# State scans of a four-layer image model: half of the products with B move to the matrix engine

## The chip, the core and the metric

The program runs on one core of a Trainium2 chip. The core has five instruction queues that run side by side: the matrix engine (PE in the profile, with PEld for its weight loads), the vector engine (DVE), the activation engine (ACT), the general engine (POOL) and SP, which here only issues transfers. Two on-chip memories matter: SBUF, which every engine can use, and PSUM, which the matrix engine writes and which DVE and ACT can read and write. The metric is device time of the whole program in microseconds. The kernel before takes 34342.57 us (median of 3 runs, 34341.05 to 34345.31).

## The reference, cut to what matters

Four layers are added one after the other to an image of 256 x 256 positions with 128 channels. Layer 1 is a selective state scan, and the change lies there. It has four scan directions (k = 0 to 3: by rows, by columns, and both backwards), 256 inner channels and 16 states for each channel, over 65536 positions:

```python
def step(h, inp):
    d_t, x_t, B_t, C_t = inp
    dA = jnp.exp(d_t[..., None] * As)
    h = dA * h + (d_t * x_t)[..., None] * B_t[:, :, None, :]
    y = jnp.einsum('bkdn,bkn->bkd', h, C_t)
    return (h, y)
```

For each channel d and state n, a = exp(delta * A) multiplies the old state, and delta * x * B is added. B and C depend on position and state alone, not on the channel. y is the sum over the 16 states of h * C.

## The kernel before

`scan_stream` does the scans. Channels lie on the 128 partitions, in two halves (dh = 0 and 1), and positions run along the free dimension. The work is cut into 512 chunks: 4 directions times 128 chunks of 512 positions. A chunk has 8 slots (NG); a slot is four states (G) of one half. Slot j has half j % 2 and states 4 * (j // 2) onwards, so halves alternate and states rise.

In every slot the engines share the work so:

- ACT computes a = exp(delta * A) for four states, 512 positions each (L787), into the PSUM tiles `das`. Two states lie behind each other in one tile, so that one scan instruction runs over both; a is set to 0 at the seam, and a one-element ACT instruction (L791) adds the second state's carry to its first product.
- DVE runs two scan instructions (L802), each over 1024 elements: a from PSUM, the products `db` from SBUF, the result `h` to SBUF.
- POOL multiplies h with C (`c_product`, L817, 2048 elements) from SBUF to SBUF.
- PE transposes and adds the four products for the chunk's y in PSUM (`sums`, L827, 16 instructions of 128 columns for a slot), two slots later.
- The products db = B * (delta * x) for a slot are one instruction of 2048 elements (`b_product`, L769): in slots 2, 4 and 6 on POOL, in the five others on DVE. For DVE delta * x lies in PSUM (`mm` for half 0, `du1` for half 1), and B, spread over all partitions by a transfer, in SBUF (`bb`). For POOL ACT copies delta * x into SBUF (`dus`, L758).

Once a chunk, delta and delta * x of the next one are made in small steps between the slots: PE (`dt`, L704; `soft_sum`, L729), ACT (`soft_abs`, `soft_exp`, `delta_copy`), and DVE (`delta_x`, L747, one instruction for each half). B and C come from PE (`xproj`), go out to DRAM (`xd_copy`), and come back in eight transfers of 1024 KB a chunk (`load_b`, `load_c`), each row repeated on all partitions.

The order on each engine is the program's order (`manual_schedule`): every engine runs its instructions in the order in which the loop at L906 issues them, and waits where data or a buffer is not ready. `h` has three buffers, `hc` three, `db` five, `bb` and `cc` three each. In PSUM, y takes two tiles of 2 KB a partition, `das` two of 4 KB, `mm` and `du1` 2 KB each.

Of the kernel before, what the change touches and what calls it, by code (L numbers as in the profile page):

```python
# [576 lines left out]
def scan_stream(c, xc2, y, w):  # L577
# [8 lines left out]
    G, BL, NG = 4, 1024, 8  # L586
    R = y[1].shape[3]
    NW = BL // S
    on_pool = (2, 4, 6)
    b_order = {0: (3,), 1: (4,), 2: (5,), 3: (6, 7), 4: (8,), 6: (10,)}  # L590
# [5 lines left out]
    with ExitStack() as a:  # L596
        st = a.enter_context(tc.tile_pool(name="l1b_st", bufs=1))
        io = a.enter_context(tc.tile_pool(name="l1b_io", bufs=2))
        bcp = a.enter_context(tc.tile_pool(name="l1b_bc", bufs=3))
        wk = a.enter_context(tc.tile_pool(name="l1b_wk", bufs=2))  # L600
        dram = a.enter_context(tc.tile_pool(name="l1b_dr", bufs=4, space=DRAM))
        ps1 = a.enter_context(tc.tile_pool(name="l1b_p1", bufs=1, space=PSUM))
        states = [st.tile([P, 2, 16], F32, name=f"l1b_state{k}") for k in range(4)]

        xds = [st.tile([64, CH], F32, name=f"l1b_xd{i}") for i in range(3)]
        for s in states:
            nc.vector.memset(s, 0.0)
        for xd in xds:
            nc.vector.memset(xd[32:64], 1.0)
        ys = [ps1.tile([P, CH], F32, name=f"l1b_y{dh}") for dh in range(2)]  # L610
        das = [ps1.tile([P, 2, CH], F32, name=f"l1b_da{i}") for i in range(2)]


        mm = ps1.tile([P, CH], F32, name="l1b_mm")
        du1 = ps1.tile([P, CH], F32, name="l1b_du")
        blocks, bcs, bbs, ccs, soft, dls, dbs, hs, hcs, yts = ({} for _ in range(10))
# [49 lines left out]

        def xproj(ch):
            if ch >= N:
                return
            k = chunks[ch][0]  # L670
            for dh in range(2):
                nc.tensor.matmul(  # L672
                    du1[:40],
                    w["xproj"][:, dh, k, :],
                    in_block(blocks[ch][0], ch, dh),
                    start=dh == 0,
                    stop=dh == 1,
                )

        def xd_copy(ch):  # L680
            if ch >= N:
                return
            xd = xds[ch % 3]
            nc.scalar.copy(xd[:40], du1[:40])
            bc = bcs[ch] = dram.tile([32, CH], F32, name="l1b_bc")
            nc.sync.dma_start(bc, xd[8:40])

        def load_b(m):
            if m < 4 * N:
                n0 = m % 4 * G  # L690
                bb = bbs[m] = bcp.tile([P, G, CH], F32, name="l1b_bb")
                nc.sync.dma_start(bb, bcs[m // 4][n0 : n0 + G][None].to_broadcast([P, G, CH]))

        def load_c(m):
            if m < 4 * N:
                n0 = 16 + m % 4 * G
                cc = ccs[m] = bcp.tile([P, G, CH], F32, name="l1b_cc")
                nc.sync.dma_start(cc, bcs[m // 4][n0 : n0 + G][None].to_broadcast([P, G, CH]))


# [11 lines left out]
        def soft_abs(ch):  # L712
            if ch >= N:
                return
            soft[ch] = wk.tile([P, CH], F32, name="l1b_tail", bufs=1)
# [17 lines left out]
        def delta_copy(ch, dh):  # L733
# [4 lines left out]
            dl = dls[ch, dh] = wk.tile([P, CH], F32, name=f"l1b_dl{dh}")  # L738
            nc.scalar.copy(dl, mm)  # L739
            af = dls[ch, dh, "first"] = wk.tile([P, 16], F32, name=f"l1b_af{dh}")  # L740
# [3 lines left out]
        def delta_x(ch, dh):  # L744
            if ch >= N:
                return
            nc.vector.tensor_tensor(  # L747
                like_block(du1 if dh else mm, ch),
# [5 lines left out]
        def du_copy(ch):  # L754
            if ch >= N:
                return
            dls[ch, "du"] = wk.tile([P, CH], F32, name="l1b_dus")
            nc.scalar.copy(dls[ch, "du"], mm)  # L758

        def b_product(g):  # L760
            ch, j = divmod(g, NG)
            if ch >= N:
                return
            db = dbs[g] = wk.tile([P, G, CH], F32, name="l1b_db", bufs=5)
            if j in on_pool:
                eng, du = nc.gpsimd, dls[ch, "du"]
            else:
                eng, du = nc.vector, du1 if j % 2 else mm
            eng.tensor_tensor(db, bbs[g // 2], du[:, None, :].to_broadcast([P, G, CH]), ALU.mult)  # L769

        def scans(g, extras):
            ch, j = divmod(g, NG)
            k, dh, n0, rev = chunks[ch][0], j % 2, j // 2 * G, chunks[ch][0] >= 2
            db = dbs.pop(g).rearrange("p g t -> p (g t)")
            h = hs[g] = wk.tile([P, G, CH], F32, name="l1b_h", bufs=3)
            hf = h.rearrange("p g t -> p (g t)")
            dl, af = dls[ch, dh], dls[ch, dh, "first"]
            mid = CH - 1 if rev else CH
            for i in range(2):
                one, two = n0 + 2 * i + rev, n0 + 2 * i + 1 - rev  # L780
                da = das[i].rearrange("p g t -> p (g t)")
                if g == 0 or ch == N // 2 and j == 0:
                    nc.vector.memset(da[:, mid : mid + 1], 0.0)
                for n in (one, two):
                    o = n % 2 * CH
                    lo, hi = (0, CH) if n == one else (0, CH - 1) if rev else (1, CH)
                    nc.scalar.activation(  # L787
                        da[:, o + lo : o + hi], dl[:, lo:hi], AF.Exp, scale=w["A"][:, k, dh, n : n + 1]
                    )
                first = db[:, 2 * i * CH + mid : 2 * i * CH + mid + 1]  # L790
                nc.scalar.activation(  # L791
                    first,
                    states[k][:, dh, two : two + 1],
                    AF.Identity,
                    scale=af[:, two : two + 1],
                    bias=first,
                )
                sl = slice(2 * i * CH, 2 * i * CH + 2 * CH)
                h_, a_, d_ = hf[:, sl], da, db[:, sl]
                if rev:  # L800
                    h_, a_, d_ = h_[:, ::-1], a_[:, ::-1], d_[:, ::-1]
                nc.vector.tensor_tensor_scan(  # L802
                    h_, a_, d_, states[k][:, dh, one : one + 1], ALU.mult, ALU.add
                )
# [4 lines left out]

        def keep_state(g):  # L810
            ch, j = divmod(g, NG)
            k, dh, n0 = chunks[ch][0], j % 2, j // 2 * G
            nc.scalar.copy(states[k][:, dh, n0 : n0 + G], hs[g][:, :, 0 if k >= 2 else CH - 1])  # L813

        def c_product(g):
            hc = hcs[g] = wk.tile([P, G, CH], F32, name="l1b_hc", bufs=3)
            nc.gpsimd.tensor_tensor(hc, hs[g], ccs[g // 2], ALU.mult)  # L817
            hs.pop(g - 1, None)

        def y_turn(ch, dh):  # L820
            if ch < 0:
                return
            yt = yts[dh] = wk.tile([P, CH], F32, name="l1b_yt", bufs=1)
            nc.scalar.copy(yt, ys[dh])  # L824

        def turned(to, b, part, start, stop):
            nc.tensor.matmul(  # L827
                to[:, bass.ts(b, P)],
                part,
                c.ident,  # L830
                start=start,
                stop=stop,
                is_transpose=True,
                skip_group_check=True,
            )

        def y_start(ch, dh):
            k = chunks[ch][0]
            xc, yo = blocks[ch]
            for b in range(CH // P):  # L840
                if k == 2:
                    turned(ys[dh], b, in_block(yo, ch, dh)[:, bass.ts(b, P)], b == 0, True)
# [10 lines left out]
        def sums(g):  # L853
            ch, j = divmod(g, NG)
            new = chunks[ch][0] % 2 == 1
            if j < 2 and not new:
                y_start(ch, j)
            hc = hcs.pop(g)
            for i in range(G):
                for b in range(CH // P):  # L860
                    turned(
                        ys[j % 2], b, hc[:, i, bass.ts(b, P)], new and j < 2 and i + b == 0, True
                    )

        def y_back(ch, dh):
# [6 lines left out]
            for b in range(CH // P):  # L872
                turned(ys[dh], b, yts[dh][:, bass.ts(b, P)], b == 0 and not add, True)
# [17 lines left out]
        for m in range(3):  # L891
            load_b(m)
            load_c(m)
        for dh in range(2):
# [6 lines left out]
            if dh == 0:  # L901
                du_copy(0)
            b_product(dh)
        b_product(2)
        load_b(3)
        for ch in range(N):  # L906
            nxt = ch + 1
            for s in range(NG):
                g = NG * ch + s
                if s == 3 and ch % 2 == 0:  # L910
                    load_y(ch + 2)
                if s == 5 and ch % 2 == 1:
                    load_x(ch + 3)
                if s == 4:
                    delta_x(nxt, 0)
                for j in b_order.get(s, ()):
                    b_product(NG * ch + j)
                extras = [[], []]
                if s == 1:
                    extras = [  # L920
                        [lambda: y_turn(ch - 1, 0), lambda: y_back(ch - 1, 0)],
                        [lambda: soft_abs(nxt), lambda: y_out(ch - 1, 0)],
                    ]
                if s == 2:
                    extras = [
                        [lambda: y_turn(ch - 1, 1), lambda: y_back(ch - 1, 1)],
                        [lambda: soft_exp(nxt), lambda: y_out(ch - 1, 1)],
                    ]
                if s == 3:
                    extras[1] = [lambda: delta_copy(nxt, 0)]  # L930
                if s == 4:
                    extras[0] = [lambda: du_copy(nxt)]
                if s == 5:
                    extras = [[lambda: soft_abs(nxt)], [lambda: soft_exp(nxt)]]
                if s == 6:
# [860 lines left out]
```

## Time and profile before

The profiled execution took 34336.33 us, of which its span covers 34334.6. Its scan stage runs from the first scan instruction (3912.9 us) to the end of the last one (29617.4 + 2.3 us): 25706.8 us, or 50.21 us for each of 512 chunks. What is left, 8629.5 us, is the other layers and the ends of layer 1.

| engine, whole span | busy us | share | instructions |
|---|---|---|---|
| PE | 23728.7 | 69% | 108660 |
| DVE | 31153.8 | 91% | 23679 |
| ACT | 23345.7 | 68% | 48143 |
| POOL | 27466.5 | 80% | 6996 |

A line of the profile's groups names the source line, the engine, the operation, what it writes and reads, its shape and its count; after the bar stand busy time in us and the mean duration of one in ns, and then the time for which the engine stood idle just before such instructions, with what ended it. Busy time counts overlapped parts of neighbouring instructions once, so busy time over count is the pace in a row, a little under the mean duration.

### The profile page before, as it was taken

How to read it: one execution, taken by the hardware profiler on the slowest of the kernel's cores; microseconds unless marked ns; L12 is line 12 of the kernel's file. 1: busy time of each engine (PE TensorE's matmuls, PEld its weight loads, DVE VectorE, ACT ScalarE, POOL GpSimd, SP SyncE). 2: the span in 40 equal slices, each digit the busy share in tenths (PEclk: the TensorE clock that was granted, in tenths of full speed). 3: DMA queues.
4: the chain of work that ended last, by engine and by line, in shares of the span. 5: the costliest groups of instructions: out<-in, count | busy, mean ns of one | idle time of the engine just before them, and what ended most of it. 6: DMA issues, size and time to landing. Idle time of an engine off the chain costs nothing. (4 is left out here: it accounts for less than half of the span.)

```text
span 34334.6 us, 330861 instructions
## 1 busy us (share of the span) xinstructions
PE 23728.7 (69%) x108660; PEld 15714.0 (46%) x108660; DVE 31153.8 (91%) x23679; ACT 23345.7 (68%) x48143; POOL 27466.5 (80%) x6996
## 2 busy tenths in 40 slices
PE   7999766666666666666666666666666666799877
PEld 3554444444444444444444444444444444434444
DVE  6668999999999999999999999999999999873699
ACT  3667777777777777777777777777777777532477
POOL 2446899999999999999999999999999999720000
PEclk9999877777777777777777777777887787899999
DMA  3113455555555555555555555555555555675111
GB/s 141 45 45 123 185 190 189 191 190 190 189 191 189 189 190 190 190 189 191 195 201 199 201 200 200 199 202 200 200 202 200 201 199 201 209 233 160 68 35 33
DMA packets 2076823, 5952.61 MB, mean 173 GB/s; under 512 B 115207, under 2 KB 1379608, under 8 KB 1499222
## 3 DMA queue, kind: packets, MB, share of 16 engines
q1 hardware_dynamic: 1939122, 5860.18, 47.2%
q10 hardware_dynamic: 135972, 71.27, 0.7%
q8 instruction: 855, 14.01, 0.2%
q14 instruction: 874, 7.16, 0.1%
HBM read 5238.41 MB, written 692.58 MB: 173 GB/s over the span
## 5 line engine op out<-in xcount | busy, mean ns | idle before, releaser
L802 DVE TENSOR_TENSOR_SCAN l1b_h<-l1b_da,l1b_state,l1b_db 128x1024 f32<-128x1024 f32 x8192 | 18847.8, 2337 | 678.8 <-ACT l1b_db L791 594.3
L817 POOL TENSOR_TENSOR l1b_hc<-l1b_h,l1b_cc 128x2048 f32<-128x2048 f32 x4096 | 18480.3, 4537 | 430.8 <-DVE l1b_h L802 430.8
L787 ACT ACTIVATE l1b_da<-l1b_dl,l_alog 128x512 f32<-128x512 f32 (+1 forms) x16384 | 11298.8, 690 | 2793.1 <-DVE l1b_h L802 2484.9
L827 PE MATMUL l1b_y<-ident,l1b_hc 128*128 128x128 f32 x65536 | 10636.3, 331 | 3479.7 <-POOL l1b_hc L817 3474.4
L827 PEld LDWEIGHTS l1b_y<-ident,l1b_hc 128*128 128x128 f32 x65536 | 9760.0, 175 | 5869.2 <-POOL l1b_hc L817 4330.6
L769 POOL TENSOR_TENSOR l1b_db<-l1b_bb,l1b_dus 128x2048 f32<-128x2048 f32 x1536 | 6965.5, 4535 | 46.6 <-DMA l1b_bb<-l1b_bc 46.6
L769 DVE TENSOR_TENSOR l1b_db<-l1b_bb,l1b_du 128x2048 f32<-128x2048 f32 x2048 | 4656.9, 2274 | 35.1
L704 PE MATMUL l1b_mm<-l1b_xd,l_dtw 41*128 41x512 f32 x2048 | 1753.9, 950 | 3303.1 <-ACT l1b_dus L758 2746.7
L791 ACT ACTIVATE l1b_db<-l1b_state,l1b_db,l1b_af 128x1 f32<-128x1 f32 x8192 | 3045.4, 372 | 0.0
L813 ACT COPY l1b_state<-l1b_h 128x4 f32<-128x4 f32 x4095 | 788.9, 193 | 2387.2 <-DVE l1b_h L802 2386.4
L729 PE MATMUL l1b_mm<-l1b_tail,ident 128*128 128x512 f32 x2048 | 1470.0, 808 | 911.4 <-ACT l1b_tail L724 908.9
L704 PEld LDWEIGHTS l1b_mm<-l1b_xd,l_dtw 41*128 41x128 f32 x2048 | 438.1, 266 | 3576.6 <-ACT l1b_dus L758 2867.5
L332 POOL TENSOR_TENSOR l0b_e<-l0b_e,l0b_den 128x1024 f32<-128x1024 f32 x512 | 969.0, 1893 | 1372.9 <-DVE l0b_den L331 726.4
L827 PE MATMUL l1b_y<-ident,l1b_yt 128*128 128x128 f32 x4096 | 877.7, 352 | 1448.2 <-ACT l1b_yt L824 1448.2
L827 PEld LDWEIGHTS l1b_y<-ident,l1b_yt 128*128 128x128 f32 x4096 | 597.2, 177 | 1890.0 <-ACT l1b_yt L824 1709.1
L758 ACT COPY l1b_dus<-l1b_mm 128x512 f32<-128x512 f32 x512 | 299.6, 585 | 1387.7 <-DVE l1b_db L769 1387.3
L769 DVE TENSOR_TENSOR l1b_db<-l1b_bb,l1b_mm 128x2048 f32<-128x2048 f32 x512 | 1171.0, 2287 | 18.2 <-ACT l1b_dus L758 0.7
L672 PE MATMUL l1b_du<-l1b_xc,l_xproj 128*40 128x512 f32 x2048 | 1158.0, 694 | 32.4 <-DMA l1b_xc<-l_xc 31.6
L308 DVE CUSTOM_DVE_ANT_0 l0b_e<-l0b_sc,l0b_bias 128x256 f32<-128x256 f32 x2048 | 745.4, 420 | 414.8 <-PE l0b_sc L297 411.4
L323 ACT ACTIVATE l0b_e<-l0b_e,l0b_top 128x256 f32<-128x256 f32 x2048 | 1012.1, 498 | 0.9 <-DVE l0b_top L308 0.9
L739 ACT COPY l1b_dl<-l1b_mm 128x512 f32<-128x512 f32 x1024 | 587.6, 574 | 520.4 <-DVE l1b_du L747 516.1
L729 PEld LDWEIGHTS l1b_mm<-l1b_tail,ident 128*128 128x128 f32 x2048 | 386.9, 237 | 1069.6 <-ACT l1b_tail L724 1065.5
(282 smaller groups left out, 30409.0 us busy)
## 6 DMA issues: line engine op xcount, KB each, us to landing
l1b_bb<-l1b_bc SPq DMA_DIRECT2D x2048, 1024.0 KB
l1b_cc<-l1b_bc SPq DMA_DIRECT2D x2048, 1024.0 KB
l1b_xc<-l_xc SPq DMA_DIRECT2D x128, 1024.0 KB
l_y<-l1b_yo SPq DMA_DIRECT2D x128, 1024.0 KB
l1b_xc<-l_xct SPq DMA_DIRECT2D x256, 512.0 KB
l_y<-l1b_yo SPq DMA_DIRECT2D x256, 512.0 KB
l_xc<-l1a_o SPq DMA_DIRECT2D x64, 1024.0 KB
l_xct<-l1a_ot SPq DMA_DIRECT2D x16, 4096.0 KB
```

Of the source, the lines that this page charges most:

```text
L323: nc.scalar.activation(e[:, i], e[:, i], AF.Exp, scale=-1.0, bias=top[:, i : i + 1], accum_out=den[:, i : i + 1],)
L332: nc.gpsimd.tensor_tensor(e, e, den[:, :, None].to_broadcast([P, 4, S]), ALU.mult)
L672: nc.tensor.matmul(du1[:40], w["xproj"][:, dh, k, :], in_block(blocks[ch][0], ch, dh), start=dh == 0, stop=dh == 1,)
L704: nc.tensor.matmul(mm, w["dt"][:, chunks[ch][0], dh * P : dh * P + P], xds[ch % 3][0:41], start=True, stop=True,)
L729: nc.tensor.matmul(mm, c.ident, soft.pop(ch), start=False, stop=True, skip_group_check=True)
L769: eng.tensor_tensor(db, bbs[g // 2], du[:, None, :].to_broadcast([P, G, CH]), ALU.mult)
L787: nc.scalar.activation(da[:, o + lo : o + hi], dl[:, lo:hi], AF.Exp, scale=w["A"][:, k, dh, n : n + 1])
L791: nc.scalar.activation(first, states[k][:, dh, two : two + 1], AF.Identity, scale=af[:, two : two + 1], bias=first,)
L802: nc.vector.tensor_tensor_scan(h_, a_, d_, states[k][:, dh, one : one + 1], ALU.mult, ALU.add)
L813: nc.scalar.copy(states[k][:, dh, n0 : n0 + G], hs[g][:, :, 0 if k >= 2 else CH - 1])
L817: nc.gpsimd.tensor_tensor(hc, hs[g], ccs[g // 2], ALU.mult)
L827: nc.tensor.matmul(to[:, bass.ts(b, P)], part, c.ident, start=start, stop=stop, is_transpose=True, skip_group_check=True,)
```

## The change

In each chunk, states 4 to 7 and 12 to 15 (q = 1 and 3, where q numbers the groups of four states) get their products with B from PE. The slots are put in a new order, in which a slot with products from a DVE or POOL instruction (q even) and one with products from PE (q odd) alternate; slot s of a chunk is `SLOTS[s]`, a pair (q, dh).

- For a slot with q odd, `fill` issues eight matmuls. The stationary operand is delta * x, turned so that positions are on partitions (`duts`; turned by PE in `du_turn`, copied by ACT in `du_copy`). The moving operand is `diag`: for 64 positions a diagonal pattern with the four values of B at each position. The result, 128 channels x 64 positions x 4 states, lands in the PSUM tile `dbt` with the four states next to each other at each position. `dbt` takes 8 KB of PSUM a partition and has one buffer.
- The pattern is made by transfers: B is turned by PE (`b_turn`), copied by ACT (`b_copy`), written to the diagonal places of a DRAM tile (`far`) in four transfers of 16-byte pieces a chunk, and loaded back (`load_d`, two of 512 KB a chunk) for the next chunk but one.
- The scans of a slot with q odd are four of 512 elements instead of two of 1024: a from SBUF (`dad`), products from `dbt` at every fourth element, h to SBUF. There is no seam, so no one-element ACT instruction.
- The scans of a slot with q even stay two of 1024, but a (`das`) now lies in SBUF beside db.
- delta * x is written to SBUF (`dus`) for both halves. The four product instructions that remain a chunk are two on DVE (for slots 4 and 0) and two on POOL (for slots 6 and 2). B's broadcast loads fall from four to two a chunk.
- `hc` has two buffers instead of three, `bb` two, `db` three.

```diff
-    on_pool = (2, 4, 6)
-    b_order = {0: (3,), 1: (4,), 2: (5,), 3: (6, 7), 4: (8,), 6: (10,)}
+    SLOTS = [(0, 0), (1, 0), (0, 1), (1, 1), (2, 0), (3, 0), (2, 1), (3, 1)]
+    HQ = P // 2
+    NB = CH // P
...
+        das = [st.tile([P, 2, CH], F32, name=f"l1b_das{i}") for i in range(2)]
+        dad = [st.tile([P, CH], F32, name=f"l1b_dad{i}") for i in range(4)]
+        dus = [st.tile([P, CH], F32, name=f"l1b_du{dh}") for dh in range(2)]
+        duts = [st.tile([P, NB, P], F32, name=f"l1b_dut{dh}") for dh in range(2)]
+        diag = {q: st.tile([P, NB, HQ, G], F32, name=f"l1b_diag{q}") for q in (1, 3)}
...
-        das = [ps1.tile([P, 2, CH], F32, name=f"l1b_da{i}") for i in range(2)]
+        dbt = ps1.tile([P, CH, G], F32, name="l1b_dbt")
         mm = ps1.tile([P, CH], F32, name="l1b_mm")
-        du1 = ps1.tile([P, CH], F32, name="l1b_du")
+        mi = ps1.tile([P, CH], F32, name="l1b_mi")
...
+        def load_d(ch, q):
+            if ch < N:
+                nc.sync.dma_start(diag[q], far[q, ch % 3])
...
             nc.vector.tensor_tensor(
-                like_block(du1 if dh else mm, ch),
+                like_block(dus[dh], ch),
                 like_block(mm, ch),
...
+        def b_product(ch, s, eng):
             if ch >= N:
                 return
...
+            q, dh = SLOTS[s]
+            db = dbs[NG * ch + s] = wk.tile([P, G, CH], F32, name="l1b_db", bufs=3)
+            du = dus[dh][:, None, :].to_broadcast([P, G, CH])
+            eng.tensor_tensor(db, bbs[ch, q], du, ALU.mult)
+
+        def fill(g):
+
+            s = g % NG
+            q, dh = SLOTS[s]
+            v = dbt.rearrange("p (a r q e) n -> p a r e q n", r=2, q=HQ, e=2)
+            for n in range(2 * NB):
+                b, r = n // 2, n % 2
+                rows = slice(r * HQ, r * HQ + HQ)
+                nc.tensor.matmul(
+                    v[:, b // 2, r, b % 2],
+                    duts[dh][rows, b],
+                    diag[q][rows, b],
...
+                if q % 2 == 0:
+                    both_scans(g, i)
+                else:
+                    for j in (2 * i, 2 * i + 1):
+                        da, n = dad[j], n0 + j
+                        nc.scalar.activation(da, dl, AF.Exp, scale=w["A"][:, k, dh, n : n + 1])
+                        h_, a_, d_ = h[:, j], da, dbt[:, :, j]
+                        if rev:
+                            h_, a_, d_ = h_[:, ::-1], a_[:, ::-1], d_[:, ::-1]
+                        nc.vector.tensor_tensor_scan(
+                            h_, a_, d_, states[k][:, dh, n : n + 1], ALU.mult, ALU.add
+                        )
...
+                if s == 0:
...
+                    fill(g + 1)
+                    du_turn(ch, 1)
...
+                if s == 2:
+                    fill(g + 1)
...
+                if s == 3:
+                    b_product(ch, 4, nc.vector)
...
                 if s == 4:
                     delta_x(nxt, 0)
...
+                    fill(g + 1)
...
+                if s == 5:
                     extras = [
...
+                        [lambda: soft_abs(nxt)],
+                        [lambda: du_copy(nxt, 0), lambda: soft_exp(nxt)],
                     ]
...
                 if s == 6:
+                    fill(g + 1)
...
                 if s == 7:
...
+                    extras = [
+                        [lambda: delta_x(nxt, 1), lambda: b_product(nxt, 0, nc.vector)],
+                        [lambda: delta_copy(nxt, 1), lambda: b_copy(ch + 2)],
+                    ]
+                    b_turn(ch + 2)
                 scans(g, extras)
...
+                sums(g - 2)
+                if s == 4:
+                    b_product(ch, 6, nc.gpsimd)
+                if s == 7:
+                    b_product(nxt, 2, nc.gpsimd)
                 c_product(g)
```

`both_scans` holds the old body of `scans` unchanged, with `das` and `db` as its operands. `extras[i]` are run behind the first or the second half of a slot's scans.

## The prediction

> **What bounds the kernel now.** I read the scan stage alone, since the change touches nothing else: 50.21 us for each of 512 chunks, with 8629.5 us of the profiled execution's 34336.33 around it. First the busy time of the engines in a stretch of that stage (the columns after the stretch are its length, then busy us with instruction counts for PE, PEld, DVE, ACT and POOL, then the granted clock, DMA share and GB/s), then the groups.
>
> ```profile
> 10000.00:16000.00 6000.00, 3730.82 (x17800) 2759.12 (x17801) 5831.01 (x2749) 4319.71 (x8844) 5900.48 (x1315) 0.74 0.53 190
> ```
>
> ```profile
> L802 DVE TENSOR_TENSOR_SCAN l1b_h<-l1b_da,l1b_state,l1b_db 128x1024 f32<-128x1024 f32 x8192 | 18847.8, 2337 | 678.8 <-ACT l1b_db L791 594.3
> L817 POOL TENSOR_TENSOR l1b_hc<-l1b_h,l1b_cc 128x2048 f32<-128x2048 f32 x4096 | 18480.3, 4537 | 430.8 <-DVE l1b_h L802 430.8
> ...
> L769 POOL TENSOR_TENSOR l1b_db<-l1b_bb,l1b_dus 128x2048 f32<-128x2048 f32 x1536 | 6965.5, 4535 | 46.6 <-DMA l1b_bb<-l1b_bc 46.6
> L769 DVE TENSOR_TENSOR l1b_db<-l1b_bb,l1b_du 128x2048 f32<-128x2048 f32 x2048 | 4656.9, 2274 | 35.1
> ```
>
> DVE is busy for 97% of the stretch and POOL for 98%. Two engines bound the stage together, so work must leave both. By busy time over count: a scan 2.30 us, a C product 4.51, a B product 4.53 on POOL and 2.28 on DVE, `delta_x` (L747) 0.67. A chunk is then 16 x 2.30 + 5 x 2.28 + 2 x 0.67 = 49.5 us on DVE and 8 x 4.51 + 3 x 4.53 = 49.7 on POOL.
>
> The last thing to see is how steady these two engines are beside each other. For one line of code, minimum, median and maximum duration in ns:
>
> ```profile
> L802 DVE TENSOR_TENSOR_SCAN l1b_h<-l1b_da,l1b_state,l1b_db x8192: 2319/2343/2354, 3912.9 to 29617.4; 128x1024 f32<-128x1024 f32 x200
> ```
>
> The spread over 8192 scans is 35 ns, although POOL runs nearly without pause. Every DVE instruction of this stage streams one operand from PSUM (`das`, `du1`, `mm`) and one from SBUF. Further on, where layer 1 ends, the trace has a DVE instruction (L1100) with two streams from SBUF, and POOL sometimes runs an add (L1029) at the same time. Its 256 instances take 737/744/2049 ns (minimum, median, maximum). Three looks at one meeting, in order of time; the second figure is the duration:
>
> ```profile
> 29826.09 1.54 POOL L1029 TENSOR_TENSOR l1c_y<-l1c_y,l1c_yt 128x512 f32<-128x512 f32 x1 [7.80 <-DMA l1c_y<-l_y]
> ...
> 29826.51 1.68 DVE L1100 SCALAR_TENSOR_TENSOR l1c_y<-l1c_y,l1c_lnb,l1c_sz 128x512 f32<-128x512 f32 x1
> ```
>
> ```profile
> 29828.10 2.02 DVE L1100 SCALAR_TENSOR_TENSOR l1c_y<-l1c_y,l1c_lnb,l1c_sz 128x512 f32<-128x512 f32 x1
> ```
>
> ```profile
> 29826.09 6.91 POOL L1029 TENSOR_TENSOR l1c_y<-l1c_y,l1c_yt 128x512 f32<-128x512 f32 x4 [7.80 <-DMA l1c_y<-l_y]
> ```
>
> The first DVE instruction starts inside POOL's first add and ends 0.56 us after that add's end (29827.63). The second takes 2.02 us and ends at about 29830.1, 0.5 us after POOL's second add. POOL's four adds take 6.91 us; two undisturbed ones take 3.01 (at 29815.28), so four would be 6.02, and each DVE instruction cost POOL 0.44 us. They take turns: each holds the other off for a whole instruction. In the same place L1093, with one stream from PSUM, keeps 732/740/748.
>
> **The change part by part.** *DVE.* Removed are three of five B products (6.8 us a chunk) and eight long scans (18.4); added are sixteen scans of 512. No row has these. Products of 512 and 1024 elements (682 and 1216 ns in layer 3) put 0.148 us on an instruction, so a half scan is (2.30 - 0.148) / 2 + 0.148 = 1.22 us; below, 1.15 (half of 2.30); above, 2.30, if reading every fourth PSUM element gains nothing from the smaller count. I take 1.22, as length is all that the rows show to matter. DVE's own sum is 8 x 2.30 + 16 x 1.22 + 2 x 2.28 + 2 x 0.67 = 43.8 us.
>
> *POOL.* One B product goes: 8 x 4.51 + 2 x 4.53 = 45.1 us.
>
> *What moves with it.* `dbt` needs the PSUM that held `das` and `du1`. So the eight long scans that stay, with `das` and db, and DVE's two B products, with `bb` and `dus`, become instructions with two SBUF streams. That is L1100's case, and POOL reads SBUF in all its ten instructions. The half scans (`dad` from SBUF, `dbt` from PSUM) and `delta_x` (`mm` in PSUM) stay in L802's case. If ten DVE instructions exclude ten POOL instructions, the chunk can't be under 45.1 + 8 x 2.30 + 2 x 2.28 = 68.1 us, whatever the order.
>
> *Slot by slot*, with DVE first in an even slot because `c_product` of the slot before waits for a semaphore of the last half scan:
>
> - Slots 0, 2 and 6: scan, C product, scan: 2.30 + 4.51 + 2.30 = 9.11 each.
> - Slots 1 and 5: four half scans, 4.88, with a C product of 4.51 beside them.
> - Slot 3: DVE's product first, POOL held: 2.28 + 4.88 = 7.16.
> - Slot 4: `delta_x` goes first, so POOL's C product of slot 3 gets in ahead of the scan; then scan, POOL's B product, scan: 4.51 + 2.30 + 4.53 + 2.30 = 13.64.
> - Slot 7: two half scans and `delta_x` (3.11) lie under a C product (4.51), then DVE's product, then POOL's with two half scans beside it: 4.51 + 2.28 + 4.53 = 11.32.
>
> The sum is 27.33 + 9.76 + 7.16 + 13.64 + 11.32 = 69.2. Were a hand-over as cheap as L1100's (0.44 us against 0.68 alone, so 0.24 less), ten of them would save 2.4: 66.8. I take 68.0.
>
> The Trainium skill ("SBUF — State Buffer", Who interferes with whom) says that any VectorE instruction with two SBUF inputs contends with a GpSimd instruction that reads SBUF, and that whoever starts first keeps the shared port for the whole instruction. By that rule nothing of an instruction overlaps, and the sum is 69.2; by the trace's meeting, where part does, 66.8. The rule names scans by implication only, and the trace shows none.
>
> *PE.* In the stretch of 6000 us, 119.5 chunks, it is busy 3730.82 / 119.5 = 31.2 us a chunk. A fill has 256 columns; L704 with 512 takes 1753.9 / 1024 = 1.71 us, so a fill costs 0.86 and 32 cost 27.4; twelve more turnings at 0.16 (10636.3 / 65536) add 2. Together 60.6 us, under 68. A slot's eight fills, 6.9 us, must end within the even slot before, 9.11: hidden, with 2.2 to spare. `sums`, queued behind them, then runs into the odd slot, where POOL's next product doesn't need it.
>
> *ACT.* Eight one-element instructions of 0.37 us go, one copy of 0.58 and `b_copy` (at most 0.58) come: no matter. In slot 5 the list before the third half scan (0.20 + two of 0.58 + two of 0.69 = 2.74) is later than two half scans (2.44) by 0.3.
>
> *SP and DMA.* Six loads of 1024 KB and two of 512 replace eight of 1024, and four scattered writes a chunk come. Issues take SP 0.3 to 0.5 us each. `load_c` for q = 3, then `load_d`, stand behind the C product of slot 2, which frees their buffer; the data is wanted three slots later. Hidden; uncovered, a load would cost the 5 to 10 us of a slot.
>
> *Sum:* 8629.5 + 512 x 68.0 = 43445 us. The set-up (two DVE memsets, six 512 KB writes) is some tens of us at most, once. The profiled execution lies 6 us under the median, so nothing is corrected: 43450.
>
> **The rivals.** *Scans don't take turns with POOL* (one stream is slow enough, or only L1100's kind of instruction does). Against it: L1100's kind differs only in its arithmetic. For it: no scan with two SBUF streams is in the trace. POOL would bound at 45.1 us, or 49.7 if the two products still exclude it; with 47 the time is 8629.5 + 24064 = 32690, faster. It decides if POOL's products keep near 4.5 us beside the even slots. This also covers the change doing what its words promise.
>
> *Fills end late.* If a write to PSUM in pieces of four elements with gaps doubles a fill to 1.72 us, eight take 13.8, 4.7 more than their cover, four times a chunk: 68.0 + 18.8 = 86.8, so 53070 us. It decides above 1.14 us a fill. Nothing in the trace shows PE writing so. The skill ("PSUM — Partial Sum Buffer", Specifications) says that non-contiguous PSUM patterns slow matmuls significantly, with no figure.
>
> *Strided reading slows the half scans* to the 2.30 of a long one: sixteen times 1.08 more, 68.0 + 17.3 = 85.3, so 52300 us. Against it: a scan needs 2.1 ns for an element (2.30 less 0.148, over 1024), twice what a product needs, so reading is not what paces it.
>
> **How the numbers follow.** Taking turns 0.84, no turns for scans 0.11, the two slow cases 0.05 together. The likeliest gives 43450. Its low end: both sides of each turn save 0.24, 68.1 - 4.8 = 63.3 with no gap left: 41040. Its high end: each odd slot loses one half scan's time to ACT or PE, 69.2 + 4 x 1.2 = 74.0: 46520. I give it 0.96 of that case, so it holds 0.96 x 0.84 = 0.81 of all. Under 0.2% (69 us) the measurement of this kernel can't tell a difference: faster 0.11, same 0.01, slower 0.88.
>
> **What would show it.** Right: about half of the scans of 1024 near 4.51 + 2.30 = 6.8 us, POOL's products stretched to as much, the stage near 68 us a chunk; half scans steady near 1.2. Wrong: both of them steady at 2.3 and 4.5; or DVE idle before half scans with PE's fills as what ended it; or half scans over 1.5.

## The result and the profile after

The changed kernel takes 43125.46 us (median of 4 runs, 43124.57 to 43131.31) against 34341.81 before (4 runs): 1.2558 times as long, 95% interval 1.2537 to 1.2580. The forecast was 43450, slower. The scan stage lasts from 3903.4 us to the end of the last half scan at 38411.9, 67.40 us a chunk instead of 50.21; the forecast's chunk was 68.0.

The same stretch of the scan stage as before, in the changed kernel (length, then busy us and instructions of PE, PEld, DVE, ACT and POOL, then clock, DMA share, GB/s):

```profile
10000.00:16000.00 6000.00, 3603.82 (x20538) 2667.89 (x20538) 5847.87 (x2494) 2947.12 (x6054) 5105.52 (x890) 0.78 0.37 126
```

DVE looks as busy as before (97%), and POOL less (85%). Neither figure shows what happened, since an instruction that is held off counts as busy. The groups show it, by mean duration after the bar:

```profile
L912 POOL TENSOR_TENSOR l1b_hc<-l1b_h,l1b_cc 128x2048 f32<-128x2048 f32 x4096 | 22806.3, 5581 | 5112.5 <-DVE l1b_h L899 2634.8
L899 DVE TENSOR_TENSOR_SCAN l1b_h<-l1b_das,l1b_state,l1b_db 128x1024 f32<-128x1024 f32 x4096 | 20540.6, 5052 | 499.9 <-ACT l1b_db L888 497.2
...
L861 DVE TENSOR_TENSOR_SCAN l1b_h<-l1b_dad,l1b_state,l1b_dbt 128x512 f32<-128x512 f32 x8192 | 9828.1, 1253 | 373.2 <-PE l1b_dbt L836 234.2
L836 PE MATMUL l1b_dbt<-l1b_diag,l1b_dut 64*128 64x256 f32 x32768 | 5779.9, 510 | 5749.9 <-DVE l1b_h L861 5743.1
```

A long scan, 2337 ns before, now has a mean of 5052 ns, and POOL's product with C went from 4537 to 5581. Both run the instruction that they ran before; the scan alone has its a in SBUF instead of PSUM. By busy time over count DVE's chunk is 8 x 5.01 for long scans, 16 x 1.20 for half scans, 2 x 2.96 for products and 2 x 0.66 for `delta_x`: 66.5 us. With the long scans at 2.30 and the products at 2.28, as in the kernel before, it would be 43.5. The other 23.0 us a chunk are DVE being held off.

The single lines of the long scans, of POOL's products with C and of the half scans (minimum, median, maximum in ns):

```profile
L899 DVE TENSOR_TENSOR_SCAN l1b_h<-l1b_das,l1b_state,l1b_db x4096: 2314/6333/6697, 3903.4 to 38400.6; 128x1024 f32<-128x1024 f32 x196
```

```profile
L912 POOL TENSOR_TENSOR l1b_hc<-l1b_h,l1b_cc x4096: 4502/6143/6667, 3912.0 to 38412.0; 128x2048 f32<-128x2048 f32 x196
```

```profile
L861 DVE TENSOR_TENSOR_SCAN l1b_h<-l1b_dad,l1b_state,l1b_dbt x8192: 1243/1249/1283, 3911.9 to 38410.6; 128x512 f32<-128x512 f32 x200
```

An undisturbed long scan still takes 2314 ns, so SBUF does not make a scan slower in itself. The median is 4.0 us longer, most of a POOL product, and POOL's median is 1.6 us over its minimum: more than half of each are held off by the other engine. The half scans, with one stream from PSUM, are nearly as steady as the scans before. One meeting of DVE and POOL in order of time (start, duration; the first line holds two POOL products in a row):

```profile
15030.01 10.99 POOL L912 TENSOR_TENSOR l1b_hc<-l1b_h,l1b_cc 128x2048 f32<-128x2048 f32 x2
```

```profile
15036.81 6.34 DVE L899 TENSOR_TENSOR_SCAN l1b_h<-l1b_das,l1b_state,l1b_db 128x1024 f32<-128x1024 f32 x1
```

```profile
15040.96 6.52 POOL L912 TENSOR_TENSOR l1b_hc<-l1b_h,l1b_cc 128x2048 f32<-128x2048 f32 x1
```

```profile
15043.07 6.56 DVE L899 TENSOR_TENSOR_SCAN l1b_h<-l1b_das,l1b_state,l1b_db 128x1024 f32<-128x1024 f32 x1
15049.56 2.26 DVE L826 TENSOR_TENSOR l1b_db<-l1b_bb,l1b_du 128x2048 f32<-128x2048 f32 x1
```

The first scan starts inside the second of the two POOL products, which ends near 15041.0 (15030.01 + 10.99), and itself ends 2.1 us later. The POOL product behind it starts at 15040.96 and takes 6.52 us: 4.51 of its own and 2.0 for the scan. The second scan waits for that product's end at 15047.48 and ends 2.15 us after it. They go in turn, as in the meeting that the forecast read from the end of layer 1.

### The profile page after: what moved, and what is told of

Read it like the earlier page. It is cut to its first block, busy times and chain, and to the rows that moved or that the text cites. A ratio compares the mean times of both kernels' runs of the same rounds, so it can differ in the third digit from the quotient of the medians.

```text
span 43129.3 us, 410111 instructions
## 1 busy us (share of the span) xinstructions
PE 28415.7 (66%) x147572; PEld 19089.5 (44%) x147572; DVE 39807.5 (92%) x26241; ACT 21786.7 (51%) x45071; POOL 31572.7 (73%) x6484
## 4 chain that ended last, share of the span: by engine, by line
DVE 38%; POOL 19%; PE 17%; ACT 10%; issue 10%; DMA 0%; SPq 0%; DVEq 0%; POOLq 0%; ACTq 0%
DVE l1b_h L899 19%; POOL l1b_hc L912 12%; DVE l1b_h L861 8%; POOL l1b_db L826 6%; PE l1b_y L683 6%; DVE l1b_db L826 4%; PE l1b_mi L703 2%; PE l1b_dbt L836 2%; ACT l1b_dad L857 2%; DVE l1b_du L804 1%; DVE l1a_mm L522 1%; ACT l1b_das L884 1%; PE l2f_fp L1498 1%; PE l2f_op L1505 1%; ACT l1b_tail L781 1%
## 5 line engine op out<-in xcount | busy, mean ns | idle before, releaser
L912 POOL TENSOR_TENSOR l1b_hc<-l1b_h,l1b_cc 128x2048 f32<-128x2048 f32 x4096 | 22806.3, 5581 | 5112.5 <-DVE l1b_h L899 2634.8
L899 DVE TENSOR_TENSOR_SCAN l1b_h<-l1b_das,l1b_state,l1b_db 128x1024 f32<-128x1024 f32 x4096 | 20540.6, 5052 | 499.9 <-ACT l1b_db L888 497.2
L861 DVE TENSOR_TENSOR_SCAN l1b_h<-l1b_dad,l1b_state,l1b_dbt 128x512 f32<-128x512 f32 x8192 | 9828.1, 1253 | 373.2 <-PE l1b_dbt L836 234.2
L836 PE MATMUL l1b_dbt<-l1b_diag,l1b_dut 64*128 64x256 f32 x32768 | 5779.9, 510 | 5749.9 <-DVE l1b_h L861 5743.1
L836 PEld LDWEIGHTS l1b_dbt<-l1b_diag,l1b_dut 64*128 64x128 f32 x32768 | 4048.2, 253 | 6882.6 <-DVE l1b_h L861 6008.4
L826 POOL TENSOR_TENSOR l1b_db<-l1b_bb,l1b_du 128x2048 f32<-128x2048 f32 x1024 | 6660.4, 6504 | 46.7 <-DVE l1b_du L804 46.7
L857 ACT ACTIVATE l1b_dad<-l1b_dl,l_alog 128x512 f32<-128x512 f32 x8192 | 5439.6, 712 | 0.0
L884 ACT ACTIVATE l1b_das<-l1b_dl,l_alog 128x512 f32<-128x512 f32 (+1 forms) x8192 | 5435.1, 712 | 0.7
L703 PE MATMUL l1b_mi<-l1b_xc,l_xproj 128*40 128x512 f32 x2048 | 1826.2, 1047 | 4013.4 <-ACT l1b_dut L818 3988.1
L826 DVE TENSOR_TENSOR l1b_db<-l1b_bb,l1b_du 128x2048 f32<-128x2048 f32 x1024 | 3029.9, 2959 | 0.0
L761 PE MATMUL l1b_mm<-l1b_xd,l_dtw 41*128 41x512 f32 x2048 | 1342.3, 741 | 0.0
```

What stands on the lines that cost most here:

```text
L703: nc.tensor.matmul(mi[:40], w["xproj"][:, dh, k, :], in_block(blocks[ch][0], ch, dh), start=dh == 0, stop=dh == 1,)
L761: nc.tensor.matmul(mm, w["dt"][:, chunks[ch][0], dh * P : dh * P + P], xds[ch % 3][0:41], start=True, stop=True,)
L826: eng.tensor_tensor(db, bbs[ch, q], du, ALU.mult)
L836: nc.tensor.matmul(v[:, b // 2, r, b % 2], duts[dh][rows, b], diag[q][rows, b], start=True, stop=True, skip_group_check=True,)
L857: nc.scalar.activation(da, dl, AF.Exp, scale=w["A"][:, k, dh, n : n + 1])
L861: nc.vector.tensor_tensor_scan(h_, a_, d_, states[k][:, dh, n : n + 1], ALU.mult, ALU.add)
```

## The experiments

Each time below is also given as a chunk: time less 8629.5 us, over 512. Where one run was timed, the kernel before ran beside it (34345.3, 34325.6 and 34334.5 us in the three sets).

**Does the operands' place alone make the loss?** Three kernels leave the kernel before as it is, without matmuls for products and without strided reading, and only move operands from PSUM to SBUF (two of them give up a buffer to make room). First one of its two tiles of a:

```diff
-        das = [ps1.tile([P, 2, CH], F32, name=f"l1b_da{i}") for i in range(2)]
+        das = [(st, ps1)[i].tile([P, 2, CH], F32, name=f"l1b_da{i}") for i in range(2)]
...
-            dls[ch, "du"] = wk.tile([P, CH], F32, name="l1b_dus")
+            dls[ch, "du"] = wk.tile([P, CH], F32, name="l1b_dus", bufs=1)
```

> The kernel before, with one of its two PSUM tiles of a moved to SBUF, so that the first long scan of every slot (8 of 16 a chunk) reads two SBUF streams; nothing goes to PE. (The copy of delta * x for POOL gets one buffer instead of two, to make room.) Taking turns with POOL: POOL's 49.7 us a chunk plus eight scans at 2.06 to 2.30 us gives 66.2 to 68.1 us a chunk, 42520 to 43500 us in all, as long as the whole change; scans with both streams in SBUF near 4.5 + 2.3 us, the others at 2.34. A scan that is only slower from SBUF, whatever POOL does, would show one duration for all of them and less than 10 us a chunk. If the matmuls or the strided reading cost the time, this kernel stays at 34340.

Measured: 43230.8 us, 67.58 us a chunk, within 0.3% of the whole change. The scans' line in this kernel:

```profile
L802 DVE TENSOR_TENSOR_SCAN l1b_h<-l1b_da,l1b_state,l1b_db x8192: 2315/2349/6655, 3896.1 to 38519.5; 128x1024 f32<-128x1024 f32 x200
```

The half of the instances that still read a from PSUM keep 2.3 us, so the median stays there; the maximum is close to that of the changed kernel (6697). Then both tiles:

```diff
-        das = [ps1.tile([P, 2, CH], F32, name=f"l1b_da{i}") for i in range(2)]
+        das = [st.tile([P, 2, CH], F32, name=f"l1b_da{i}") for i in range(2)]
...
-            hc = hcs[g] = wk.tile([P, G, CH], F32, name="l1b_hc", bufs=3)
+            hc = hcs[g] = wk.tile([P, G, CH], F32, name="l1b_hc", bufs=2)
```

> The same with both tiles of a in SBUF: all 16 long scans of a chunk read two SBUF streams. (The products with C get two buffers instead of three, to make room.) Taking turns: 49.7 + 16 x 2.06 to 2.30 = 82.7 to 86.5 us a chunk, 50970 to 52920 us: twice the loss of the kernel with half of them. If the loss came from a fixed wait per slot and not from each instruction, it would not double. If scans are not concerned: 34340.

Measured: 51349.2 us, 83.44 us a chunk. Over the kernel before, eight scans cost 17.4 us a chunk and sixteen cost 33.2: 2.17 and 2.08 us a scan. The loss goes by the instruction, not by the slot. Then only the operand of DVE's products:

```diff
+        du1s = st.tile([P, CH], F32, name="l1b_du1s")
...
-                like_block(du1 if dh else mm, ch),
+                like_block(du1s if dh else mm, ch),
...
-                eng, du = nc.vector, du1 if j % 2 else mm
+                eng, du = nc.vector, du1s if j % 2 else mm
```

> The kernel before, with delta * x of half 1 written to SBUF instead of PSUM: four of DVE's five products with B a chunk read two SBUF streams, all scans keep a in PSUM. Taking turns: 49.7 + 4 x 2.04 to 2.28 = 57.9 to 58.8 us a chunk, 38270 to 38740 us. If only scans are concerned, or the loss of the change lies elsewhere: 34340.

Measured: 38302.4 us, 57.95 us a chunk, 1.93 us for each of the four products. In this kernel (L770 holds the products, L803 the scans):

```profile
L770 DVE TENSOR_TENSOR l1b_db<-l1b_bb,l1b_du1s x2048: 2260/3768/8232, 3909.6 to 33556.3; 128x2048 f32<-128x2048 f32 x187
...
L770 DVE TENSOR_TENSOR l1b_db<-l1b_bb,l1b_mm x512: 2286/2289/2289, 3899.4 to 33510.0; 128x2048 f32<-128x2048 f32 x171
```

```profile
L803 DVE TENSOR_TENSOR_SCAN l1b_h<-l1b_da,l1b_state,l1b_db x8192: 2316/2336/2353, 3916.0 to 33582.9; 128x1024 f32<-128x1024 f32 x200
```

One operation, one engine, one size: with delta * x in SBUF it waits, with delta * x in PSUM (`mm`) its 512 instances lie within 3 ns. The scans of this kernel, with a in PSUM again, are undisturbed.

**Is it what POOL reads?** In the changed kernel the product with C is replaced by zeros written as often as keeps POOL busy, and a product of a few positions that keeps its wait:

```diff
-            nc.gpsimd.tensor_tensor(hc, hs[g], ccs[ch, SLOTS[s][0]], ALU.mult)
+            cc = ccs[ch, SLOTS[s][0]]
+            for _ in range(3):
+                nc.gpsimd.memset(hc, 0.0)
+            nc.gpsimd.tensor_tensor(hc[:, :, 0:4], hs[g][:, :, 0:4], cc[:, :, 0:4], ALU.mult)
```

> The changed kernel, leaving out the product with C (all but 4 of 512 positions): in its place POOL writes zeros into the same tile three times, which reads nothing, then multiplies those few positions, so that it still waits for the scans. POOL stays busy for several us a slot. If it is POOL's reading of SBUF that holds DVE off, the long scans fall to 2.3 us but for those that meet POOL's two remaining products with B, and the chunk falls to between DVE's own 43.8 us plus a little and 43.8 plus two holds near 3.3, 44 to 50.4 us: 31200 to 34430 us. If any busy POOL, or the order of the slots, holds DVE, the scans stay near 6 us and the time above 40000. If PE, ACT or the transfers of the new scheme are a second bound, it shows here as a time above 34430 with short scans.

Measured: 37632.8 us, 56.65 us a chunk: outside the expectation, by my own sizing. One write takes 1.81 us, so three and the small product make POOL's sum 8 x (3 x 1.81 + 0.39) + 2 x 4.53 = 55.6 us, and POOL is the bound, at 97% of the stretch. The long scans' median fell to 2343 ns all the same. The same with two writes:

> As the kernel whose POOL writes zeros in place of the product with C (the product is left out but for 4 of 512 positions), with two writes of 1.81 us a slot instead of three, since three made POOL the bound: POOL's own sum is 8 x (2 x 1.81 + 0.39) + 2 x 4.53 = 41.2 us a chunk, under DVE's 43.8. If what held DVE off was POOL's reading alone, the chunk now falls to 44 to 50.4 us (43.8 us, and up to two holds near 3.3 by the two products with B that POOL still makes): 31160 to 34430 us, at or under the kernel before. If the new scheme has a second bound (PE's fills, ACT's order, the transfers), DVE stands idle for it and the time stays above 34430.

Measured: 33502.5 us, 48.58 us a chunk. Its long scans and its POOL writes:

```profile
L899 DVE TENSOR_TENSOR_SCAN l1b_h<-l1b_das,l1b_state,l1b_db x4096: 2315/2335/6651, 3904.4 to 28771.1; 128x1024 f32<-128x1024 f32 x196
```

```profile
L914 POOL MEMSET l1b_hc<- 128x2048 f32 x1976 | 3565.8, 1805 | 58.8 <-PE l1b_y L683 2.0
```

POOL is busy for 98% of the stretch here, more than in the changed kernel, and writes for 3565.8 of the 6000 us, yet the scans beside it are short. The writes do not hold DVE off. The longest scan still waits 4.3 us (6651 less 2315), which fits the two products with B that POOL still makes. So what counts is that POOL reads, and not that it is busy; all of POOL's reading instructions here have two streams from SBUF, so one with a single stream was not tried. The kernel also shows that PE's fills, ACT's order and the transfers of the new scheme can run at 48.6 us a chunk: no second bound above that hides under the first.

**Fewer of the long scans with two SBUF streams.** In the changed kernel, PE's tile is cut to two states and one tile of a moves into the room:

```diff
-        dbt = ps1.tile([P, CH, G], F32, name="l1b_dbt")
+        dbt = ps1.tile([P, CH, 2], F32, name="l1b_dbt")
+        das = [(ps1, st)[i].tile([P, 2, CH], F32, name=f"l1b_das{i}") for i in range(2)]
...
-            v = dbt.rearrange("p (a r q e) n -> p a r e q n", r=2, q=HQ, e=2)
+            v = dbt.rearrange("p (r a q e) n -> p a r e q n", r=2, q=HQ, e=2)
...
-                    diag[q][rows, b],
+                    diag[q][rows, b, :, 0:2],
...
-                        h_, a_, d_ = h[:, j], da, dbt[:, :, j]
+                        h_, a_, d_ = h[:, j], da, dbt[:, :, j % 2]
```

> The changed kernel with PE's product tile cut to two states (this leaves out products: states 2 and 3 of each group of four use those of states 0 and 1, and positions are not in their places), which frees room for one of the two tiles of a in PSUM: four of the eight long scans of a chunk have one SBUF stream again. Taking turns: 4 x 2.06 to 2.30 us less, 58.2 to 59.2 us a chunk, 38430 to 38940 us. If the loss is in the even slots as such, not in the instruction's two streams, the time stays near 43100.

Measured: 38136.4 us, 57.63 us a chunk, 9.8 us less for four scans. That is 0.8% under the expectation's low end; the smaller fills, or an order with fewer gaps, may be the rest, which was not tried apart.

**All four products on DVE.**

```diff
-        b_product(0, 2, nc.gpsimd)
+        b_product(0, 2, nc.vector)
...
-                    b_product(ch, 6, nc.gpsimd)
+                    b_product(ch, 6, nc.vector)
...
-                    b_product(nxt, 2, nc.gpsimd)
+                    b_product(nxt, 2, nc.vector)
```

> The changed kernel with all four products with B a chunk on DVE, none on POOL. Taking turns: the two engines' instructions add up, so a product of 4.53 us on POOL becomes one of 2.28 on DVE, twice a chunk: 67.4 - 4.5 = 62.9 us a chunk, 40820 us in all, although DVE, the busier engine by the page (92%), gets more work. If DVE were the bound by its own work, it would be 2 x 2.28 longer: 45460. If POOL alone were, 2 x 4.53 shorter: 38490.

Measured: 41513.8 us, 64.23 us a chunk. The sign is that of turns, and neither rival is near, but 3.2 us a chunk came back and not 4.5. The stretch in this kernel:

```profile
10000.00:16000.00 6000.00, 3757.86 (x21434) 2772.84 (x21434) 5992.95 (x2801) 3094.63 (x6349) 4203.40 (x747) 0.80 0.39 132
```

DVE has no gap left, while POOL stands idle for 30%. The expected 62.9 took over whatever gaps the changed kernel has. With 2.0 us for each DVE instruction that excludes POOL (6.52 - 4.51 in the meeting above), the excluding instructions need 8 x 4.51 + 12 x 2.0 = 60.1 us here, so 4.1 us a chunk are left over, against 2.3 in the changed kernel (45.1 + 10 x 2.0 = 65.1 of 67.4). They hold gaps in which neither engine excludes the other, and scans that meet an idle POOL and so cost their whole 2.30; the two were not measured apart.

**A wait taken from POOL.** The changed kernel shows one that the forecast had not seen. Who POOL waited for in it, in us, times and the longest:

```profile
POOL l1b_hc L912 <- DVE l1b_h L899: 2634.8, 1118, 4.7
POOL l1b_hc L912 <- PE l1b_y L683: 2076.2, 488, 5.1
```

On PE the projection in slot 5 waits for an ACT copy, the sums of slot 3 stand behind it, and POOL, with two output buffers, waits for them: 2076.2 / 512 = 4.1 us a chunk. The edit lets the sums go first:

```diff
-                if s == 5:
-                    xproj(ch + 2)
...
                 sums(g - 2)
+                if s == 5:
+                    xproj(ch + 2)
```

> The changed kernel with one call moved on PE: in slot 5 the sums of slot 3 come before the projection (which waits for an ACT copy), no longer behind it. That takes away POOL's wait of about 4 us a chunk for PE to free its output tile. If the time is the sum of the instructions that exclude one another, a POOL wait that lies beside DVE's long scans is worth little: 0 to 1 us a chunk, 42610 to 43130 us. If POOL's wait lies on the path that sets the end, 4 us a chunk come back: about 41080.

Measured: 43044.7 us, 1.2537 times the kernel before (1.2501 to 1.2573; two runs). That is 81 us under the changed kernel, 0.16 us a chunk, and the intervals overlap. POOL's waits in it:

```profile
POOL l1b_hc L912 <- DVE l1b_h L899: 5488.6, 1884, 4.9
...
POOL l1b_hc L912 <- PE l1b_y L683: 498.2, 163, 4.9
```

The wait for PE fell by 1578 us and the one for DVE's scans grew by 2854. Taking this wait away gave almost nothing back: POOL's idle time only changed its name.

## Why the prediction was right

- *DVE and POOL take turns* was the forecast's step for the sign and the size, and it is shown: from the kernel before by moving operands alone (b_das_half, b_das_sbuf, b_du_sbuf), and from the changed kernel by taking POOL's reads away (a_pool_writes2). That scans are concerned, which no row had shown, is settled too.
- *The sum of 68.0 us a chunk* was 67.4, by two small errors against each other; that they nearly cancel is luck, and the mechanism is not. A turn is cheaper than the two values between which the forecast chose its 68.0: a scan of 2.30 us costs POOL 6.52 - 4.51 = 2.0 us, not 2.06 or 2.30. So the excluding instructions alone need some 45.1 + 10 x 2.0 = 65.1 (a product on DVE counted like a scan), and 2.3 us are left for gaps in which neither engine excludes the other and for scans that meet an idle POOL. The forecast's floor of 68.1 us, "whatever the order", did not hold: the measured chunk lies 0.7 us under it, since the instructions overlap by 0.3 us at a turn.
- *Slot by slot* the forecast was wrong. In slot 2 POOL is a product further behind than I laid out, and the slot's two scans take 12.82 us and not 9.11; in slot 6 they take only 4.59, back to back while POOL waits for PE. The sum comes out near all the same, since what excludes one another adds up in any order, but for the gaps. Slots 5 and 6 on DVE:

```profile
15002.40 4.76 DVE L861 TENSOR_TENSOR_SCAN l1b_h<-l1b_dad,l1b_state,l1b_dbt 128x512 f32<-128x512 f32 x4
15008.14 4.59 DVE L899 TENSOR_TENSOR_SCAN l1b_h<-l1b_das,l1b_state,l1b_db 128x1024 f32<-128x1024 f32 x2 [0.97 <-ACT l1b_db L888]
```

- *DVE's own work* was forecast at 43.8 us and is 43.5; a half scan at 1.22, and is 1.20 (all 8192 within 1243 to 1283 ns). So the rival of strided reading falls: reading every fourth PSUM element costs a scan nothing that these rows show.
- *PE* was mis-sized: 60.6 us a chunk forecast, 3603.82 / 89.0 = 40.5 measured. A fill's matmul (each has two records in the trace, 32768 for 16384) costs 5779.9 / 16384 = 0.35 us and not 0.86. The rival of late fills falls: DVE's idle time before half scans put down to PE is 234.2 us in all, under 0.5 us a chunk. Whether the broken pattern in PSUM slows a fill at all, as the page on PSUM that the prediction quotes would have it, no run here separates. The forecast's cover for the fills was wrong too: it took 9.11 us for every even slot, and slot 6 has 4.59, under the 6.9 us forecast for eight.
- *ACT* was foreseen to be late by 0.3 us before the third half scan of slot 5. There DVE has no wait: its four half scans take 4.76 us in a row. The wait comes in slot 6, where DVE stands 0.97 us a chunk for the carry (497.2 / 512). POOL's wait of 4.1 us a chunk for PE, behind another ACT copy of slot 5, was not foreseen; taking it away gave 0.16 us a chunk.
- *The rule of the Trainium skill* ("SBUF — State Buffer", Who interferes with whom), that a DVE instruction with two SBUF inputs contends with a POOL instruction that reads SBUF and not with one that only writes it, agrees with the runs: products hold scans off, writes (1.81 us each) don't. That the first keeps the port for the whole instruction, the page says of DVE's two-port modes; the prediction carried it over to this case. By it the sum was 69.2, and the measured 67.4 is nearer to the 66.8 by the trace's meeting, where part of an instruction overlaps; both sums rest on the slots as laid out, which came otherwise.

What was not tried is a version with PE's products and all of a in PSUM. Both kernels lay out 16 KB of PSUM a partition. PE's products and all of a would take that alone, and y, `mm` and `mi` need another 8: it needs another staging. No kernel here that computes the whole result beats the kernel before.

## What to carry to other kernels

Before an operand moves from PSUM to SBUF to make room, count the streams of the instruction that reads it: a DVE instruction with two SBUF streams and a POOL instruction that reads SBUF excluded one another in every run here, and where both engines are full their times add. Look for one meeting of such a pair anywhere in the trace, price it, and then sum the excluding instructions; what the order added to that sum came to 2.3 and 4.1 us of 67.4 and 64.2 here. A busy share counts being held off as work, so read minimum, median and maximum instead.

## What the hardware showed beyond that

Matmuls on 64 of 128 rows, alternating between the two halves of the rows and writing to different places in PSUM, ran at 0.35 us for 256 fp32 columns, while 512 columns on 41 rows take 1342.3 / 1024 = 1.31 us in the same kernel (L761): half the columns for about a quarter of the time. The runs don't separate the side-by-side halves from the clock and from gaps between instructions. An exponential of 512 elements that ACT writes to SBUF has a mean of 712 ns, against 690 into PSUM.
